# Layer 0 of a two-layer image kernel: the skip term and two products move to GpSimd

## The chip, the cores and the metric

The kernel runs on one core of one Trainium2 chip, in float32 throughout. The metric is the device time of one execution in microseconds (us). A core has TensorE (PE; its weight loads are listed apart as PEld), VectorE (DVE), ScalarE (ACT), GpSimd (POOL) and SyncE (SP), whose queue issues the DMAs. Each engine runs its own instructions in order; between engines, semaphores hold an instruction back until its data or its buffer is there.

## The reference, cut to what matters

The input is x, 8 images of 64 x 64 positions and 192 channels. Layer 0 normalizes it, applies a depthwise 3x3 convolution with a residual, a LayerNorm, a Mamba-2 style mixer (below), a second depthwise convolution, a LayerNorm and an MLP of width 768 with GELU; the result is added to x. Layer 1 is a selective scan in four directions over 384 channels and 16 states. Only layer 0's mixer is touched:

```python
xBC = silu(causal_conv1d(xBC, conv1d_w, conv1d_b))
xm = xBC[..., :DIN].reshape(B, L, NH, HD)      # 6 heads of 64
Bm, Cm = ...                                   # 64 states each
# inside a chunk, per head:
scores = (Cm_i . Bm_j) * exp(cs_i - cs_j) * dt_j   (j <= i)
y      = scores @ xm
states = sum_j Bm_j * (dt_j * decay_last_j) * xm_j
y      = y + (Cm @ carried state) * exp(cs)
y = y + xm * D_skip[None, None, :, None]
y = y.reshape(B, L, DIN) * silu(z)
```

## The kernel before

Layer 0 cuts each image's 4,096 positions into 8 tiles of 512 tokens, 64 tiles in all, and each tile into 4 chunks of 128 tokens. In most of layer 0 channels lie on partitions and tokens run along the free dimension; in the mixer tokens lie on partitions.

The order of the instructions is not written out by hand. Each stage is a Python generator (`mlp`, `norm2`, `conv2`, `output`, `mixer`, `states`, `turn`, `scores`, `powers` and so on) that yields steps with an engine and a cost (`step("DVE", 0.55, ...)`), takes and gives back buffers by name (`yield "take", "sm"`), and waits for events (`yield "wait", ("e", T, c)`). The planner `Flow` picks at every turn the step that could start soonest by those costs, plus a small rank per stage, and records it. The order that results is fixed on every engine. When a cost, a buffer or a step changes, the planner lays the whole of layer 0 in a new order; it knows nothing of engines that slow each other.

What stands around the change:

- `convolve` leaves `cv`, the 384 channels of xm for a tile, channels on partitions.
- `turn` (p_t, L698) transposes a chunk of `cv` by three PE transposes into a PSUM tile of the `sm` pool (3 buffers). DVE reads that tile twice: `xdt` = x*dt (L704) and `xw` = x*w (L709), with dt and w broadcast over the 64 columns of a head. Each has one buffer. Then the PSUM tile is given back.
- `states` multiplies the carried state with C (p_i, L739), scales it on DVE into `t1` (the trace calls it `t`, L741, one buffer), and makes the chunk's new state from `xw` (p_n, L750), with a decay and an add on DVE (L760, L763).
- `mixer` sums y in PSUM (p_y): three matmuls of `cv` with `dsk`, diagonal matrices of D (L786), then for each head a matmul of the scores `e` with `xdt` (L789). An fp32 matmul is two instructions in the trace. DVE adds `t1` (L802) and multiplies by silu(z) (`zs`, L805). The first chunk of an image has no carried state and no add.
- GpSimd holds the sums over two channel groups in the LayerNorms (`s`, L365), the residual sum `xr<-xr,x` (L923, one a tile) and small edge copies. DVE holds the two 3x3 convolutions (L343), 16 `scalar_tensor_tensor` instructions each per tile, and the causal convolution (L497), 12 per tile.

Layer 1 runs after layer 0 and shares nothing with it but the images in DRAM.

Of the kernel before, what the change touches and what calls it, by code (L numbers as in the profile page):

```python
# [8 lines left out]
F32 = mybir.dt.float32  # L9
# [13 lines left out]
NH, HD, NS = 6, 64, 64  # L23
DIN = 384
# [29 lines left out]
def bc(ap, axis, shape):  # L54

    return ap.unsqueeze(axis).to_broadcast(shape)
# [128 lines left out]
def step(engine, weight, do, after=None, table=None):  # L185
    return engine, weight, do, after, table


def layer0(tc, consts, x, x1s, mv1, w_in, w_out, w_fc1, w_fc2, rows):
    nc = tc.nc  # L190
    ident, low, up, grp, eps, ones96, ones1, p96, p128 = consts
    v96 = {k: p96[:, s] for k, s in C96.items()}
    v128 = {k: p128[:, s] for k, s in C128.items()}
# [8 lines left out]
    with ExitStack() as ctx:  # L202
# [32 lines left out]
        nc.vector.tensor_add(fb1, ps[:, 0:6], v128["fb1"])  # L235
        for ct in range(CT):
            nc.vector.tensor_scalar_mul(wf1[:, ct], wf1[:, ct], v96["l2w"][:, ct : ct + 1])
        rv = wp.tile([128, 12], F32, name="rv")
        nc.sync.dma_start(out=rv, in_=rows.partition_broadcast(128))
        dtb, an = rv[:, 0:6], rv[:, 6:12]  # L240
        nc.scalar.activation(an, an, AF.Exp)
        nc.vector.tensor_scalar_mul(an, an, -1.0)

        for i in range(3):
            nc.vector.tensor_scalar_mul(wo[:, i], wo[:, i], v128["rms"][:, i : i + 1])
        dsk = wp.tile([128, 3, 128], F32, name="dsk")
        for i in range(3):
            nc.vector.tensor_scalar_mul(dsk[:, i], ident, v128["dsk"][:, i : i + 1])

        xins = [wp.tile([CP, CT, RT + 2, WI + 2], F32, name=f"xin{i}") for i in range(2)]  # L250
        xxs = [xxp.tile([CP, CT, RT + 2, WI + 2], F32, name=f"xx{i}", bufs=1) for i in range(3)]
# [3 lines left out]
        f = Flow(tc)  # L255
        f.LAG, f.STAY, f.RANK = 0.684, -0.464, -0.01
        for tag, n in (("mm", 5), ("sm", 3), ("xin", 2), ("xs", 3), ("h", 3), ("cin", 2), ("cv", 2), ("zs", 2),
                       ("dt", 2), ("e", 5), ("yt", 4), ("yc", 1), ("xx", 3), ("x2", 1), ("m", 1), ("sq", 1), ("s2", 1), ("ld", 3), ("csr", 1), ("xdt", 1), ("xw", 1), ("t1", 1)):
            f.pool(tag, n)
        got = {}  # L260

# [422 lines left out]
        def turn():  # L684

            for T in range(len(tiles)):
                yield "wait", ("w2", T)
                yield "wait", ("cv", T)
                dt, w2, cv, bm = got["dt", T], got["w2", T], got["cv", T], got["bm", T]
                for c in range(NQ):  # L690
                    tk = slice(c * Q, c * Q + Q)
                    yield "take", "sm"
                    px = qp.tile([128, DIN], F32, name="p_t", tag="sm")
                    r = yield step(
                        "PE",
                        0.4,
                        lambda: [
                            nc.tensor.transpose(px[:, i * 128 : i * 128 + 128], cv[:, i, tk], ident) for i in range(3)  # L698
                        ],
                    )  # L700
                    yield "take", "xdt"
                    xdt = got["xdt", T, c] = ch.tile([128, DIN], F32, name="xdt", bufs=1)
                    f.at["xdt", T, c] = yield step(
                        "DVE", 0.55, lambda: [nc.vector.tensor_mul(hv(xdt), hv(px), bc(dt[:, c], 2, heads))], r  # L704
                    )
                    yield "take", "xw"
                    xw = got["xw", T, c] = ch.tile([128, DIN], F32, name="xw", bufs=1)
                    r = yield step(
                        "DVE", 0.55, lambda: [nc.vector.tensor_mul(hv(xw), hv(px), bc(w2[:, c], 2, heads))], r  # L709
                    )  # L710
                    f.give("sm", r)
                    yield "take", "sm"
                    pb = qp.tile([128, DIN], F32, name="p_b", tag="sm")
                    q = yield step("PE", 0.2, lambda: [nc.tensor.transpose(pb[:, :NS], bm[:, tk], ident[:NS, :NS])], 0.0)
                    f.fork(keep_b(T, c, pb, q, r))
# [52 lines left out]
        def mixer():  # L768

            for T, (b, t) in enumerate(tiles):  # L770
                yield "wait", ("cv", T)
                cv = got["cv", T]
                ssq = got["ssq", T] = sp.tile([128, NQ], F32, name="ssq")
                for c in range(NQ):
                    tk = slice(c * Q, c * Q + Q)
                    yield "wait", ("xdt", T, c)
                    yield "wait", ("e", T, c)
                    e, xdt = got.pop(("e", T, c)), got.pop(("xdt", T, c))
                    yield "take", "sm"
                    py = qp.tile([128, DIN], F32, name="p_y", tag="sm")  # L780

                    def out():

                        for i in range(3):
                            cs = slice(i * 128, i * 128 + 128)
                            f.keep(nc.tensor.matmul(py[:, cs], cv[:, i, tk], dsk[:, i], start=i == 0, stop=False))  # L786
                        for hd in range(NH):
                            cs = slice(hd * HD, hd * HD + HD)
                            f.keep(nc.tensor.matmul(py[:, cs], e[:, hd], xdt[:, cs], start=False, stop=hd == NH - 1))  # L789

                    q = yield step("PE", 2.2, out)
                    f.give("e", q)
                    f.give("xdt", q)
                    if c == 0:
                        yield "wait", ("zs", T)
                    zs = got["zs", T]
                    yield "take", "yt"
                    yt = got["yt", T, c] = tp.tile([128, DIN], F32, name="yt", bufs=4)
                    if t or c:
                        yield "wait", ("t1", T, c)  # L800
                        t1 = got.pop(("t1", T, c))
                        q = yield step("DVE", 0.55, lambda: [nc.vector.tensor_add(yt, t1, py)])  # L802
                        f.give("sm", q)
                        f.give("t1", q)
                        q = yield step("DVE", 0.66, lambda: [nc.vector.tensor_mul(yt, yt, zs[:, c])])  # L805
                    else:
                        q = yield step("DVE", 0.55, lambda: [nc.vector.tensor_mul(yt, py, zs[:, c])])
                        f.give("sm", q)
                    sqj = ch.tile([128, DIN], F32, name="sqj", bufs=1)
                    r = yield step(  # L810
                        "ACT",
                        0.75,
                        lambda: [nc.scalar.activation(sqj, yt, AF.Square, accum_out=ssq[:, c : c + 1])],
                        q,
                    )
                f.give("zs", q)
                yield "wait", ("states", T)
                f.give("cv", q)
                f.give("dt", q)
                f.at["yt", T] = r  # L820
# [1016 lines left out]
def _layout(i):  # L1837
    import numpy as np

    g = {k: np.asarray(a) for k, a in i.items()}  # L1840
    l0 = lambda k: g["L0_conv_" + k]
    l1 = lambda k: g["L1_conv_" + k]

    def part(a, p):

        a = a.reshape(-1, p, int(np.prod(a.shape[1:])))
        return a.transpose(1, 0, 2).reshape(p, -1)

    p96 = [l0(k) for k in ("cpe1_w", "cpe1_b", "ln1_w", "ln1_b", "cpe2_w", "cpe2_b", "ln2_w", "ln2_b", "fc2_b")]
    p128 = [l0("conv1d_w"), l0("conv1d_b"), l0("rms_w"), np.repeat(l0("D_skip"), HD), l0("fc1_b")]  # L1850
    p128 += [l1(k) for k in ("conv_w", "conv_b")]

    al = l1("A_logs").reshape(K, 2 * DT, 64, NP1, 2).transpose(4, 2, 0, 3, 1)
    p128 = [part(a, 128) for a in p128]
    p128 += [part(l1("Ds"), 128), al.reshape(128, -1), part(l1("ln_gamma"), 128), part(l1("ln_beta"), 128)]
    win = l0("in_proj_w")
    wx = l1("x_proj_weight")
    out = {
        "x": g["x"].transpose(0, 3, 1, 2).reshape(g["x"].shape[0], C, L),
        "p96": np.concatenate([part(a, CP) for a in p96], 1),  # L1860
        "p128": np.concatenate(p128, 1),
        "rows": np.concatenate([l0("dt_bias"), l0("A_log")]),

        "w_in0": np.concatenate([win[:384], win[896:], win[384:896]]).T,
        "w_out0": l0("out_proj_w").T,
        "w_fc1": l0("fc1_w").T,
        "w_fc2": l0("fc2_w").T,
        "w_in1": l1("in_proj_w").T,

        "w_x": np.concatenate([wx[:, R:], wx[:, :R]], 1).transpose(2, 0, 1),  # L1870
        "w_dt": np.concatenate([l1("dt_projs_weight").transpose(0, 2, 1), l1("dt_projs_bias")[:, None]], 1),
        "w_out1": l1("out_proj_w").T,
    }
    return {k: np.ascontiguousarray(a) for k, a in out.items()}
# [18 lines left out]
```

## Time and profile before

| What | Value |
| --- | --- |
| Median of 3 runs | 23,702.0 us (23,690.56 to 23,706.31) |
| Profiled execution | 23,706.3 us; its span is the same 23,706.3 us |
| PE busy over the span | 21,012.6 us (89%) |
| DVE busy over the span | 21,257.2 us (90%) |
| ACT busy over the span | 20,961.7 us (88%) |
| POOL busy over the span | 16,001.1 us (67%) |
| First and last transposes p_t of layer 0 | 94.6 us and 4,648.5 us |

A view by windows gives each engine's busy time in a stretch of the span, with the TensorE clock granted in it. A row of a group names the source line, the engine, the operation, what it writes and reads with its shapes, how often it occurred, its busy time in us and its mean in ns, and after the second bar the idle time of the engine just before it with what ended that idle time. Busy time counts overlapping instructions of one engine once, so the mean times the count can be larger. A row of the timeline begins with the start and the length in us.

### The profile page before, as it was taken

The page shows a single profiled execution, that of the slowest core. Times are in us where ns is not written, and L with a number is a line of the kernel's source. Part 1 is how long each engine was busy: PE and PEld are TensorE (multiplying, and loading weights), DVE is VectorE, ACT ScalarE, POOL GpSimd, SP SyncE. Part 2 cuts the span into 40 slices and gives each one's busy share as a digit, 9 for nine tenths or more (in the row PEclk, how much of TensorE's full clock was granted, in tenths as well). Part 3 has the DMA queues.
Part 4 walks back from the last instruction along what each step waited for, and adds up shares of the span by engine and source line. Part 5 has one row for each costly group of instructions (what it writes and reads, how often), then busy time and mean ns, then how long its engine had stood idle before and what let it go on. Part 6 is the DMA issues. An engine that isn't in the chain of part 4 may idle for free.

```text
span 23706.3 us, 312102 instructions
## 1 busy us (share of the span) xinstructions
PE 21012.6 (89%) x100356; PEld 10233.4 (43%) x100356; DVE 21257.2 (90%) x22093; ACT 20961.7 (88%) x37466; POOL 16001.1 (67%) x12871
## 2 busy tenths in 40 slices
PE   8999999978888888888888888888888888888888
PEld 4444444434444444444444444444444444444444
DVE  7888888779998999899989998999899989998998
ACT  5666666679998999899989998999899989998998
POOL 1111111159995998599859986997699769976997
PEclk8999999989999999999999999999999999999999
DMA  1111111133233322332233233322333333333332
GB/s 51 44 44 44 45 45 46 36 101 81 82 78 112 81 81 77 110 82 81 77 108 81 81 80 111 81 81 78 108 81 82 84 102 81 82 86 100 82 82 67
DMA packets 1205983, 1859.70 MB, mean 78 GB/s; under 512 B 268960, under 2 KB 502336, under 8 KB 1195136
## 3 DMA queue, kind: packets, MB, share of 16 engines
q1 hardware_dynamic: 1204352, 1839.73, 28.5%
q8 instruction: 807, 13.22, 0.2%
q14 instruction: 824, 6.75, 0.1%
HBM read 1225.98 MB, written 210.50 MB: 61 GB/s over the span
## 4 chain that ended last, share of the span: by engine, by line
POOL 46%; PE 22%; ACT 13%; DVE 8%; issue 6%; DMA 3%; SPq 1%; POOLq 0%; ACTq 0%; DVEq 0%
POOL hc L1647 43%; ACT pw L1591 5%; ACT ea L1606 5%; POOL cy L1645 3%; PE p_f L955 3%; DVE xs L1201 2%; DMA xc<-xo 2%; PE p_x L448 2%; PE p_f L975 2%; PE y L1662 2%; PE p_o L872 1%; PE g L1617 1%; PE p_y L789 1%; PE p_d L1480 1%; PE p_z L531 1%
## 5 line engine op out<-in xcount | busy, mean ns | idle before, releaser
L1647 POOL TENSOR_TENSOR hc<-hs,cb 128x1024 f32<-128x1024 f32 x6144 | 14577.6, 2373 | 12.3 <-POOL cy L1645 10.5
L1633 DVE TENSOR_TENSOR_SCAN hs<-ea,cy,g 128x512 f32<-128x512 f32 x10752 | 13027.1, 1262 | 602.4 <-PE g L1617 408.7
L1591 ACT ACTIVATE pw<-duT,bt 128x384 f32<-128x384 f32 x16384 | 8875.4, 601 | 23.5 <-DVE duT L1538 23.5
L1606 ACT ACTIVATE ea<-dr,an 128x512 f32<-128x512 f32 x12288 | 8121.7, 709 | 186.9 <-DVE hs L1633 169.5
L1662 PE MATMUL y<-hc,sel 128*64 128x512 f32 x24576 | 6628.6, 618 | 1836.3 <-POOL hc L1647 1816.1
L1617 PEld LDWEIGHTS g<-ident,pw 128*128 128x128 f32 x49152 | 5288.2, 141 | 4335.1 <-issue 2666.3
L1617 PE MATMUL g<-ident,pw 128*128 128x128 f32 x49152 | 6788.1, 279 | 60.8 <-ACT pw L1591 29.3
L1645 POOL COPY cy<-hs 128x2 f32<-128x2 f32 x6144 | 1150.7, 187 | 3394.4 <-DMA out_x<-xl 1744.8
L1662 PEld LDWEIGHTS y<-hc,sel 128*64 128x64 f32 x24576 | 1226.6, 135 | 3250.6 <-POOL hc L1647 3025.0
L1633 DVE TENSOR_TENSOR_SCAN hs<-ea,g 128x512 f32<-128x512 f32 x1536 | 1764.2, 1203 | 160.9 <-PE g L1617 119.6
L365 POOL TENSOR_TENSOR s<-xs 96x512 f32<-96x512 f32 x64 | 121.7, 1902 | 2136.0 <-DVE xs L343 1846.6
L1201 DVE SCALAR_TENSOR_TENSOR xs<-pad,p,xs 128x4096 f32<-128x4096 f32 x192 | 860.9, 4484 | 48.0 <-ACT xs L1191 40.8
L1509 PE MATMUL p_dt<-xdbl,wd 13*128 13x512 f32 x1536 | 857.5, 639 | 41.8 <-DVE de L1522 39.9
L365 POOL TENSOR_TENSOR s<-sq 96x512 f32<-96x512 f32 x128 | 180.4, 1409 | 937.9 <-ACT sq L378 842.3
L1480 PE MATMUL p_d<-xc,wx 128*44 128x512 f32 x1536 | 788.7, 596 | 23.4 <-DMA xc<-xo 23.4
L343 DVE SCALAR_TENSOR_TENSOR x<-xx,p,x 96x512 f32<-96x512 f32 x1024 | 784.4, 815 | 15.2 <-ACT x L332 15.0
L955 PE MATMUL p_f<-h,wf 96*128 96x512 f32 x1536 | 757.2, 631 | 43.8 <-ACT zs L550 27.4
L343 DVE SCALAR_TENSOR_TENSOR xs<-xin,p,xs 96x512 f32<-96x512 f32 x1024 | 746.9, 768 | 3.6 <-ACT xs L332 3.6
L975 PE MATMUL p_f<-m,wf 128*96 128x512 f32 x1536 | 695.0, 603 | 0.0
L1531 PEld LDWEIGHTS p_du<-ident,de 128*128 128x128 f32 x3072 | 323.4, 141 | 610.1 <-DVE de L1522 406.3
L365 POOL TENSOR_TENSOR s<-x 96x512 f32<-96x512 f32 x64 | 109.1, 1704 | 690.3 <-DVE x L343 606.7
L448 PE MATMUL p_x<-h,wi 96*128 96x512 f32 x1024 | 559.4, 679 | 12.0 <-ACT h L405 12.0
(202 smaller groups left out, 19293.3 us busy)
## 6 DMA issues: line engine op xcount, KB each, us to landing
cb<-cd SPq DMA_DIRECT2D x4096, 128.0 KB
dr<-de SPq DMA_DIRECT2D x3072, 128.0 KB
xc<-xo SPq DMA_DIRECT2D x256, 768.0 KB
e<-csd SPq DMA_DIRECT2D x256, 384.0 KB
xl<-x SPq DMA_DIRECT2D x256, 384.0 KB
ut<-xo SPq DMA_DIRECT2D x128, 768.0 KB
ut<-xo SPq DMA_DIRECT2D x256, 384.0 KB
xo<-xs SPq DMA_DIRECT2D x48, 1024.0 KB
```

The source lines that it names most:

```text
L343: nc.vector.scalar_tensor_tensor(im(out[:, ct]), tap(ct, j), w[:, ct, j : j + 1], im(out[:, ct]), ALU.mult, ALU.add)
L448: nc.tensor.matmul(ps, wi[:, ct, 390 + mt * 128 : 518 + mt * 128], h[:, ct], start=ct == 0, stop=ct == 1)
L955: nc.tensor.matmul(ps, wf1[:, ct, mt * 128 : mt * 128 + 128], h[:, ct], start=ct == 0, stop=ct == 1)
L975: nc.tensor.matmul(ps[:CP], wf2[:, kt, ct * CP : ct * CP + CP], m[:, kt], start=kt == 0, stop=kt == 5)
L1201: nc.vector.scalar_tensor_tensor(xs, tap(j), kw[:, d, j : j + 1], xs, ALU.mult, ALU.add)
L1591: nc.scalar.activation(st["pw", p, j][:, :, i], st["duT"][:, j].rearrange("p (g c) -> p g c", c=64), AF.Copy, scale=st["bt"][:, j, n : n + 1],
L1606: nc.scalar.activation(ea[:, f], state[s]["dr", d][:, f], AF.Exp, scale=an[:, k, p, at : at + 1])
L1617: nc.tensor.transpose(g[:, f, j * 128 : j * 128 + 128], state[s]["pw", p, j][:, 2 * d + f].rearrange("p a b -> p (a b)"), ident,)
L1633: nc.vector.tensor_tensor_scan(rev(h[:, f]), rev(ea[:, f]), rev(g[:, f]), 0.0 if first(s) else state[s - 1]["cy"][:, p, d, f : f + 1], ALU ...
L1645: o(nc.gpsimd.tensor_copy(st["cy"][:, p, d], h[:, :, last]))
L1647: o(nc.gpsimd.tensor_mul(hc, h, bc(st["cb", p], 1, [128, 2, TT])))
L1662: o(nc.tensor.matmul(y[half[f]], sel, hc[:, f], start=p == 0 and k > 0, stop=p == NP1 - 1))
```

## The change

The transposed chunk is copied once from PSUM by ScalarE into a new SBUF tile `xr` (two buffers; the name also belongs to an unrelated tile of the second LayerNorm stage). The PSUM tile is given back after that copy. GpSimd forms `xw` and then `xdt` from `xr`, then multiplies `xr` by D in place. In `mixer` the three diagonal matmuls are gone and each head's matmul starts its own sum; GpSimd adds `t1` to `xr`, and DVE adds `xr` to the PSUM tile. The first chunk of an image now has that add as well. D is loaded as 6 further values of the broadcast row vector, and the diagonal matrices `dsk` are not built.

```diff
@@ -235,17 +235,14 @@
         nc.vector.tensor_add(fb1, ps[:, 0:6], v128["fb1"])
-        rv = wp.tile([128, 12], F32, name="rv")
+        rv = wp.tile([128, 18], F32, name="rv")
         nc.sync.dma_start(out=rv, in_=rows.partition_broadcast(128))
-        dtb, an = rv[:, 0:6], rv[:, 6:12]
+        dtb, an, skip = rv[:, 0:6], rv[:, 6:12], rv[:, 12:18]
         nc.scalar.activation(an, an, AF.Exp)
         nc.vector.tensor_scalar_mul(an, an, -1.0)
 
         for i in range(3):
             nc.vector.tensor_scalar_mul(wo[:, i], wo[:, i], v128["rms"][:, i : i + 1])
-        dsk = wp.tile([128, 3, 128], F32, name="dsk")
-        for i in range(3):
-            nc.vector.tensor_scalar_mul(dsk[:, i], ident, v128["dsk"][:, i : i + 1])
 
         xins = [wp.tile([CP, CT, RT + 2, WI + 2], F32, name=f"xin{i}") for i in range(2)]
         xxs = [xxp.tile([CP, CT, RT + 2, WI + 2], F32, name=f"xx{i}", bufs=1) for i in range(3)]
@@ -255,7 +252,7 @@
         f = Flow(tc)
         f.LAG, f.STAY, f.RANK = 0.684, -0.464, -0.01
         for tag, n in (("mm", 5), ("sm", 3), ("xin", 2), ("xs", 3), ("h", 3), ("cin", 2), ("cv", 2), ("zs", 2),
-                       ("dt", 2), ("e", 5), ("yt", 4), ("yc", 1), ("xx", 3), ("x2", 1), ("m", 1), ("sq", 1), ("s2", 1), ("ld", 3), ("csr", 1), ("xdt", 1), ("xw", 1), ("t1", 1)):
+                       ("dt", 2), ("e", 5), ("yt", 4), ("yc", 1), ("xx", 3), ("x2", 1), ("m", 1), ("sq", 1), ("s2", 1), ("ld", 3), ("csr", 1), ("xdt", 1), ("xw", 1), ("t1", 1), ("xr", 2)):
             f.pool(tag, n)
         got = {}
 
@@ -698,17 +695,23 @@
                             nc.tensor.transpose(px[:, i * 128 : i * 128 + 128], cv[:, i, tk], ident) for i in range(3)
                         ],
                     )
+                    yield "take", "xr"
+                    xr = got["xr", T, c] = ch.tile([128, DIN], F32, name="xr", bufs=2)
+                    r = yield step("ACT", 0.5, lambda: [nc.scalar.copy(xr, px)], r)
+                    f.give("sm", r)
+                    yield "take", "xw"
+                    xw = got["xw", T, c] = ch.tile([128, DIN], F32, name="xw", bufs=1)
+                    r = yield step(
+                        "POOL", 1.0, lambda: [nc.gpsimd.tensor_mul(hv(xw), hv(xr), bc(w2[:, c], 2, heads))]
+                    )
                     yield "take", "xdt"
                     xdt = got["xdt", T, c] = ch.tile([128, DIN], F32, name="xdt", bufs=1)
                     f.at["xdt", T, c] = yield step(
-                        "DVE", 0.55, lambda: [nc.vector.tensor_mul(hv(xdt), hv(px), bc(dt[:, c], 2, heads))], r
-                    )
-                    yield "take", "xw"
-                    xw = got["xw", T, c] = ch.tile([128, DIN], F32, name="xw", bufs=1)
-                    r = yield step(
-                        "DVE", 0.55, lambda: [nc.vector.tensor_mul(hv(xw), hv(px), bc(w2[:, c], 2, heads))], r
-                    )
-                    f.give("sm", r)
+                        "POOL", 1.0, lambda: [nc.gpsimd.tensor_mul(hv(xdt), hv(xr), bc(dt[:, c], 2, heads))], 0.0
+                    )
+                    f.at["xr", T, c] = yield step(
+                        "POOL", 1.0, lambda: [nc.gpsimd.tensor_mul(hv(xr), hv(xr), bc(skip, 2, heads))], 0.0
+                    )
                     yield "take", "sm"
                     pb = qp.tile([128, DIN], F32, name="p_b", tag="sm")
                     q = yield step("PE", 0.2, lambda: [nc.tensor.transpose(pb[:, :NS], bm[:, tk], ident[:NS, :NS])], 0.0)
@@ -781,14 +784,11 @@
 
                     def out():
 
-                        for i in range(3):
-                            cs = slice(i * 128, i * 128 + 128)
-                            f.keep(nc.tensor.matmul(py[:, cs], cv[:, i, tk], dsk[:, i], start=i == 0, stop=False))
                         for hd in range(NH):
                             cs = slice(hd * HD, hd * HD + HD)
-                            f.keep(nc.tensor.matmul(py[:, cs], e[:, hd], xdt[:, cs], start=False, stop=hd == NH - 1))
-
-                    q = yield step("PE", 2.2, out)
+                            f.keep(nc.tensor.matmul(py[:, cs], e[:, hd], xdt[:, cs], start=True, stop=True))
+
+                    q = yield step("PE", 1.3, out)
                     f.give("e", q)
                     f.give("xdt", q)
                     if c == 0:
@@ -796,16 +796,17 @@
                     zs = got["zs", T]
                     yield "take", "yt"
                     yt = got["yt", T, c] = tp.tile([128, DIN], F32, name="yt", bufs=4)
+                    yield "wait", ("xr", T, c)
+                    xr = got.pop(("xr", T, c))
                     if t or c:
                         yield "wait", ("t1", T, c)
                         t1 = got.pop(("t1", T, c))
-                        q = yield step("DVE", 0.55, lambda: [nc.vector.tensor_add(yt, t1, py)])
-                        f.give("sm", q)
+                        q = yield step("POOL", 1.0, lambda: [nc.gpsimd.tensor_add(xr, xr, t1)])
                         f.give("t1", q)
-                        q = yield step("DVE", 0.66, lambda: [nc.vector.tensor_mul(yt, yt, zs[:, c])])
-                    else:
-                        q = yield step("DVE", 0.55, lambda: [nc.vector.tensor_mul(yt, py, zs[:, c])])
-                        f.give("sm", q)
+                    q = yield step("DVE", 0.55, lambda: [nc.vector.tensor_add(yt, xr, py)])
+                    f.give("sm", q)
+                    f.give("xr", q)
+                    q = yield step("DVE", 0.66, lambda: [nc.vector.tensor_mul(yt, yt, zs[:, c])])
                     sqj = ch.tile([128, DIN], F32, name="sqj", bufs=1)
                     r = yield step(
                         "ACT",
@@ -1859,7 +1860,7 @@
         "p96": np.concatenate([part(a, CP) for a in p96], 1),
         "p128": np.concatenate(p128, 1),
-        "rows": np.concatenate([l0("dt_bias"), l0("A_log")]),
+        "rows": np.concatenate([l0("dt_bias"), l0("A_log"), l0("D_skip")]),
 
         "w_in0": np.concatenate([win[:384], win[896:], win[384:896]]).T,
         "w_out0": l0("out_proj_w").T,
```

## The prediction

> **What bounds the kernel now.** The change touches layer 0 only, so I first cut layer 0 out of the span. In the page's forty slices GpSimd jumps from 1 tenth to 5 and then 9 at the ninth and tenth: layer 0 fills the first eight slices, about 4,700 us of 23,706, and the rest is layer 1, where GpSimd's `hc` products carry the chain of waits (43%). Nothing of layer 1 is edited, so the stake is what a layer-0 tile takes, 64 times over.
>
> ```profile
> POOL 1111111159995998599859986997699769976997
> ```
>
> Second, the busy time by windows, over 3,600 us of even running inside layer 0. The columns are length, then busy us (and instructions) of PE, PEld, DVE, ACT, POOL, then the granted clock.
>
> ```profile
> 900.00:4500.00 3600.00, 3368.48 (x11474) 1659.46 (x11472) 2994.53 (x4989) 2411.98 (x4737) 498.93 (x413) 0.94 0.17 45
> ```
>
> Third, the groups of the same window with shapes kept apart.
>
> ```profile
> L343 DVE SCALAR_TENSOR_TENSOR x<-xx,p,x 96x512 f32<-96x512 f32 x800 | 615.6, 819 | 0.0
> L786 PE MATMUL p_y<-dsk,cv 128*128 128x128 f32 x1188 | 181.4, 291 | 7.1 <-DVE gm L676 6.5 <-ACT yc L858 0.6
> L365 POOL TENSOR_TENSOR s<-sq 96x512 f32<-96x512 f32 x100 | 142.3, 1423 | 715.4 <-ACT sq L378 652.1 <-PE p_u L849 25.9 <-PE p_g L672 21.1
> L923 POOL TENSOR_TENSOR xr<-xr,x 96x1024 f32<-96x1024 f32 x50 | 127.6, 2552 | 0.0
> L704 DVE TENSOR_TENSOR xdt<-p_t,dt 128x384 f32<-128x384 f32 x198 | 109.2, 551 | 260.1 <-PE p_y L789 260.1
> L709 DVE TENSOR_TENSOR xw<-p_t,w 128x384 f32<-128x384 f32 x197 | 107.5, 546 | 9.8 <-PE p_n L750 9.8
> L858 ACT COPY yc<-p_u 128x384 f32<-128x384 f32 x200 | 94.0, 470 | 112.7 <-PE p_u L849 112.1
> ```
>
> The tile sum `xr<-xr,x` occurs 50 times, once a tile, so a tile (4 chunks of 128 tokens) takes 3600/50 = **72.0 us**. Per tile PE is busy 67.4 us, DVE 59.9, ACT 48.2, POOL 10.0. PE idles 4.6 us a tile: it is the bound, at 0.936 of the time. DVE has 12.1 us to spare, of which 260.1/50 = 5.2 is the wait of `xdt` for the p_y matmul that still reads its only buffer.
>
> Fourth, the timeline of one stretch, for what DVE and POOL do to each other.
>
> ```profile
> 2529.89 2.81 POOL L365 TENSOR_TENSOR s<-x 96x512 f32<-96x512 f32 x1 [6.04 <-DVE x L343]
> 2531.50 2.02 DVE L681 TENSOR_TENSOR e<-e,gm 128x768 f32<-128x768 f32 x1
> 2536.21 0.94 DVE L681 TENSOR_TENSOR e<-e,gm 128x768 f32<-128x768 f32 x1
> ```
>
> The same `e*gm` takes 2.02 us while the GpSimd sum runs and 0.94 us with GpSimd idle; the sum itself takes 2.81 us where the fastest in the window takes 1.26. They exclude each other.
>
> **What the Trainium skill says.** "SBUF — State Buffer", section Who interferes with whom: a DVE instruction with two SBUF inputs contends with a GpSimd instruction that reads SBUF, and the later one blocks fully; a DVE instruction with at most one SBUF input is free of it. The trace agrees. Of the 800 `x` steps of the convolution (two SBUF inputs), 616 meet no GpSimd instruction and average 737 ns; the 102 that start while one runs average 1,368. The `xdt` product (one input in PSUM) takes 551 ns alone and 552 during GpSimd work. "GPSIMD Engine Reference", section 3.1, prices a two-input elementwise product at about 2.6 cycles an element at 1.2 GHz: an estimate of 384 x 2.6 / 1.2 = 0.83 us before overhead. Its section 1 gives GpSimd no PSUM access, which is why the copy by ScalarE has to exist; no run here shows that.
>
> **The change, part by part.** The profiled execution took 23,706.3 us, which is also its span (nothing lies around it), 4.3 above the median of 23,702.0. Sums are per tile, then times 64.
>
> PE loses 6 instructions a chunk (three 128-column matmuls, two passes each). The group's 181.4 us over 198 chunks is 0.92 us a chunk, but it overlaps its neighbours: from the first of the six to the first `e` matmul is 0.67 us in the median and 0.75 on average. I take 0.75: 3.0 us a tile, 192 us in all. Ends: 0.67 (172) and 0.92 (235). PE becomes 64.4 us.
>
> DVE loses `xdt` and `xw`. From the start of one to the start of what follows back to back is 0.467 us: 8 x 0.467 = 3.7 us a tile. The eight image-first chunks gain one add (4 us in all), and three setup instructions of 0.27 us go; both count as nothing, and no cover is needed. The 5.2 us wait for the `xdt` buffer moves to POOL's queue. It was free time of an engine that was not the bound, so I credit nothing for it.
>
> ACT gains 4 copies out of PSUM; `yc` has the same shape at 470 ns: 1.9 us. The planner's new order also holds 363 table loads instead of 319; 44 x 1.283 us / 64 = 0.9 us. ACT becomes 51.0 of 72 us; idle time covers it. Without that cover it would cost 2.8 x 64 = 179 us. The queued work behind a copy that waits for the transpose is the next decays; 21 us a tile absorb that.
>
> POOL gains `xw`, `xdt`, the skip product and the add of `t1`: 256 x 3 + 248 = 1,016 instructions, 15.9 a tile. No 128x384 product exists on POOL before. The undisturbed minima, 1.258 us for 512 elements and 2.336 for 1,024, give a slope of 2.1 ns and a fixed 0.18: **0.99 us** at 384. The page's price with that overhead gives 1.01. The broadcast operand is new; I allow 0.9 to 1.3. So POOL gets 15.7 us more, 26 of 72 before its waits: far from full.
>
> What matters is what those 15.7 us do to DVE. DVE's two-SBUF-input work is 2,142/50 = 42.8 us a tile undisturbed, POOL's existing work 8.2: together 51 of 72 us on the shared reads, after the change 67. Existing POOL work lengthens DVE instructions by 140 us over the 50 tiles, 0.34 of its own 8.2 us. By kind the share is 0.46 (`s<-sq`, released by ACT, like the new products), 0.54 (`s<-xs`), 0.33 (`xr`), 0.14 (`s<-x`). I take 0.5: 7.9 us a tile. Ends: 0.14 (2.2 us) and all (15.7). **DVE becomes 59.9 - 3.7 + 7.9 = 64.1 us** (58.4 to 71.9), as full as PE. So the change does not move work to an idle engine: 3.7 us leave DVE and about 8 come back as blocking.
>
> The new waits. `p_n` and `p_y` now wait for POOL, behind which the whole PE queue stands. By row durations the new PE order has a median of 14.5 us of PE work between a chunk's transposes and its `p_n` (lowest tenth 7.8), 16 us to `p_y`. The chain copy, `xw`, `xdt` needs 0.47 + 2 x 0.99 us and up to one 0.94 us block each, some 4 to 5 us. It is covered unless POOL's queue is stuck: the products stand in order behind `s<-xs`, which already waits 1,394.7 us in 42 waits for DVE's convolution, some 33 us each. DVE's `yt` add now waits for POOL's add of `t1`; median DVE work between them is 7.0 us, lowest tenth 3.0, against about 2 us needed, so only a few stall. The PSUM slot of the transposes is freed after one copy instead of two products, slightly earlier. The reload of the `rows` vector by 6 values, the only altered DMA, is nothing; SP's queue has no new transfer. All other instructions move, since the planner lays the whole order again from the new costs.
>
> **Putting it together.** The old 0.936 of PE held while DVE had 12 us of slack. With two engines at 64 us that block each other I take PE's busy share at 0.88, its idle share nearly doubled. That is a choice, not a measurement: 64.4/0.88 = 73.2 us a tile, 1.2 more, 77 us in all: 23,783. At 0.895 the change would be neutral.
>
> **The rivals.**
> *A, the saving lands:* DVE is blocked little because products fall on its one-input work or idle time, PE keeps 0.936, so 64.4/0.936 = 68.8 us, 3.2 less, 205 us in all: 23,501. For it: the 3,368 busy us of PE, DVE's 5.2 us of buffer wait, the 10 us of PE work that hides the POOL chain. Against it: 42.8 us a tile of exclusive DVE work.
> *B, balance:* the forecast, 23,783; its own range 23,620 to 23,930.
> *C, the shared read interface is the bound:* nearly every POOL product holds up DVE, DVE needs 71.9 us, and at the 0.936 that a bounding engine reaches here a tile takes 76.8 us, 4.8 more: +307 us, 24,013. It decides from a blocked share of about 0.75, where DVE reaches 68 us; queued products behind a blocked `s<-xs` push the same way. For it: 0.54 on `s<-xs`, 67 of 72 us on the interface. Against it: the average of 0.34.
> That the change does not take effect is excluded: the new order has 1,536 instead of 3,072 p_y matmuls and the 1,016 GpSimd ones.
>
> **The numbers.** What a measurement of this kernel can tell from no change is about 0.2%, 47 us. A has 0.27 (0.26 faster, 0.01 same), B 0.46 (0.04 faster, 0.13 same, 0.29 slower), C 0.27, all slower. Faster 0.30, same 0.14, slower 0.56. Cases of both signs hold the chance, so B's own range stands above; the range over all, 23,510 to 24,090, leaves a tenth at each end: a full A with 0.92 us a chunk, and a C with POOL products of 1.3 us.
>
> **What would show each step.** Right: over the same window of layer 0, tiles of about 73 us, PE's busy share down to 0.88, POOL's 128x384 products near 1.0 to 1.3 us, the `x` steps of the convolution above their 819 ns mean at 900 or more, DVE's busy time up although two products left it, layer 1 unchanged. Wrong: DVE busy under 59 us a tile (A), or over 68 (C); PE waiting long on `xw` or `xdt` would put the loss in POOL's queue and not in the reads.

## The result and the profile after

The changed kernel takes 23,833.36 us in the median of 4 runs (23,820.16 to 23,848.16) against 23,704.15 for the kernel before beside it: a ratio of 1.0055, 95% interval 1.0042 to 1.0069, or **129 us slower**. The forecast was 23,783, 77 us slower.

The time is lost in layer 0. From the first transposes to the last a tile takes (4,648.5 - 94.6)/63 = 72.3 us before and (4,814.4 - 95.1)/63 = 74.9 us after; the last transposes come 166 us later, the first `hc` product of layer 1 137 us later, the end 128 us later. The end of layer 0 and layer 1 give some of it back, and the rows of layer 1 are the same within a few us.

The window of 900 to 4,500 us after, with the columns as before (length, busy us and count of PE, PEld, DVE, ACT, POOL, then the granted clock):

```profile
900.00:4500.00 3600.00, 3290.65 (x9961) 1556.93 (x9959) 2961.64 (x4447) 2447.74 (x4802) 1564.45 (x1155) 0.89 0.16 43
```

The slices of GpSimd over the span, in tenths:

```profile
POOL 3444444439995999599959995998599869976997
```

GpSimd's share of layer 0 went from 0.14 to 0.43. At 74.9 us a tile the window holds 48.1 tiles: PE is busy 68.5 us of each, DVE 61.6, ACT 50.9, POOL 32.6. PE lost six instructions a chunk and is *busier* than before; the granted clock in the same row, 0.94 before and 0.89 here, says why.

The groups of that window, shapes kept apart, that answer to those shown of before:

```profile
L340 DVE SCALAR_TENSOR_TENSOR x<-xx,p,x 96x512 f32<-96x512 f32 x766 | 631.5, 876 | 0.0
L362 POOL TENSOR_TENSOR s<-sq 96x512 f32<-96x512 f32 x96 | 154.2, 1606 | 199.7 <-ACT sq L375 180.3 <-DVE x L340 9.3 <-PE p_u L850 6.5
L705 POOL TENSOR_TENSOR xw<-xr,w 128x384 f32<-128x384 f32 x191 | 366.4, 1918 | 684.0 <-PE p_n L753 428.7 <-ACT xr L700 207.0 <-DVE t L744 27.0
L710 POOL TENSOR_TENSOR xdt<-xr,dt 128x384 f32<-128x384 f32 x191 | 249.0, 1304 | 358.5 <-PE p_y L789 358.4
L804 POOL TENSOR_TENSOR xr<-xr,t 128x384 f32<-128x384 f32 x186 | 237.8, 1278 | 161.7 <-DVE t L744 156.3 <-DVE dr L544 4.3
L700 ACT COPY xr<-p_t 128x384 f32<-128x384 f32 x190 | 90.6, 477 | 188.9 <-DVE yt L806 88.1 <-PE p_t L695 86.7 <-DVE dr L544 7.9
L713 POOL TENSOR_TENSOR xr<-xr,rv 128x384 f32<-128x384 f32 x191 | 212.3, 1111 | 13.6
L806 DVE TENSOR_TENSOR yt<-xr,p_y 128x384 f32<-128x384 f32 x192 | 104.7, 546 | 209.4 <-POOL xr L804 193.3 <-PE p_u L850 8.5 <-PE p_f L956 6.1
L789 PE MATMUL p_y<-xdt,e 128*128 128x64 f32 x2304 | 323.3, 296 | 21.4 <-DVE e L678 10.7 <-POOL xdt L710 7.1 <-DVE st L766 1.3
```

The convolution's steps went from a mean of 819 to 876 ns. The new products and the add take 1.1 to 1.9 us on average, where the shortest product takes 0.82 and the shortest add 0.98. GpSimd now waits for PE, 428.7 us for `p_n` to free `xw` and 358.4 us for `p_y` to free `xdt`, and DVE waits 193.3 us for GpSimd's add. PE itself hardly waits for the products (7.1 us for `xdt`). The timeline of one stretch shows how those last two link (start and length in us, the wait in brackets):

```profile
2501.96 0.83 POOL L710 TENSOR_TENSOR xdt<-xr,dt 128x384 f32<-128x384 f32 x1 [7.73 <-PE p_y L789]
2502.87 0.83 POOL L713 TENSOR_TENSOR xr<-xr,rv 128x384 f32<-128x384 f32 x1
2503.66 1.26 POOL L362 TENSOR_TENSOR s<-x 96x512 f32<-96x512 f32 x1
2504.88 0.99 POOL L804 TENSOR_TENSOR xr<-xr,t 128x384 f32<-128x384 f32 x1
2505.90 0.56 DVE L806 TENSOR_TENSOR yt<-xr,p_y 128x384 f32<-128x384 f32 x1 [3.58 <-POOL xr L804]
...
2522.03 2.80 POOL L924 TENSOR_TENSOR xr<-xr,x 96x1024 f32<-96x1024 f32 x1
...
2522.54 5.48 DVE L494 SCALAR_TENSOR_TENSOR cv<-cin,p,cv 128x512 f32<-128x512 f32 x5
```

GpSimd stands 7.73 us for the `xdt` buffer, then works through its queue, and DVE stands 3.58 us for the add at the end of it. Below, five convolution steps, the first of them held up by the GpSimd sum above it, take 5.48 us; at the 0.66 us from start to start that they show undisturbed they take some 3.4.

The blocking falls on GpSimd too, and harder. In another stretch one product meets a row of DVE's two-input instructions:

```profile
2651.11 10.10 POOL L705 TENSOR_TENSOR xw<-xr,w 128x384 f32<-128x384 f32 x1 [0.84 <-ACT xr L700]
...
2651.62 0.94 DVE L678 TENSOR_TENSOR e<-e,gm 128x768 f32<-128x768 f32 x1
2652.49 3.39 DVE L340 SCALAR_TENSOR_TENSOR xs<-xin,p,xs 96x512 f32<-96x512 f32 x5
2655.80 0.74 DVE L494 SCALAR_TENSOR_TENSOR cv<-cin,p,cv 128x512 f32<-128x512 f32 x1
2656.47 0.74 DVE L340 SCALAR_TENSOR_TENSOR xs<-xin,p,xs 96x512 f32<-96x512 f32 x1
2657.13 3.39 DVE L494 SCALAR_TENSOR_TENSOR cv<-cin,p,cv 128x512 f32<-128x512 f32 x5
```

A two-input instruction of DVE (`h*rs`) was running when the product began. The thirteen shown start after it, none of them is lengthened, and the product ends 0.7 us after the last of them: 10.10 us instead of 0.82. Over the window, products and adds take 413 us more than their shortest times, 8.6 us a tile.

### The profile page after: what moved, and what is told of

The parts are those of the page before. It is cut to its first block, busy times and chain, and to the rows that moved or that the text cites. A ratio compares the mean times of both kernels' runs of the same rounds, so it can differ in the third digit from the quotient of the medians.

```text
span 23834.7 us, 310291 instructions
## 1 busy us (share of the span) xinstructions
PE 21029.7 (88%) x98820; PEld 10147.4 (43%) x98820; DVE 21334.5 (90%) x21586; ACT 21123.1 (89%) x37766; POOL 17450.2 (73%) x13887
## 4 chain that ended last, share of the span: by engine, by line
POOL 46%; PE 20%; ACT 14%; DVE 9%; issue 7%; DMA 3%; SPq 1%; POOLq 0%; ACTq 0%; DVEq 0%
POOL hc L1648 41%; ACT pw L1592 6%; ACT ea L1607 5%; POOL cy L1646 3%; DVE xs L1202 2%; PE p_f L956 2%; DMA xc<-xo 2%; PE y L1663 2%; PE p_f L976 2%; PE p_o L873 1%; PE g L1618 1%; PE p_d L1481 1%; PE p_x L445 1%; DVE xs L340 1%; PE p_o L1408 1%
## 5 line engine op out<-in xcount | busy, mean ns | idle before, releaser
L705 POOL TENSOR_TENSOR xw<-xr,w 128x384 f32<-128x384 f32 x256 | 464.3, 1814 | 912.5 <-PE p_n L753 589.4
L340 DVE SCALAR_TENSOR_TENSOR x<-xx,p,x 96x512 f32<-96x512 f32 x1024 | 840.8, 871 | 11.5 <-ACT x L329 11.5
L340 DVE SCALAR_TENSOR_TENSOR xs<-xin,p,xs 96x512 f32<-96x512 f32 x1024 | 837.2, 854 | 12.9 <-ACT xs L329 12.9
L710 POOL TENSOR_TENSOR xdt<-xr,dt 128x384 f32<-128x384 f32 x256 | 338.3, 1322 | 443.0 <-PE p_y L789 437.7
```

The lines of the kernel that those rows point to most:

```text
L340: nc.vector.scalar_tensor_tensor(im(out[:, ct]), tap(ct, j), w[:, ct, j : j + 1], im(out[:, ct]), ALU.mult, ALU.add)
```

## The experiments

All differences are against the kernel before, timed beside them (23,703 to 23,704 us). "Lengthening" is what DVE's instructions take above the undisturbed time of their own kind while a GpSimd instruction runs, summed over the window and given per tile: 2.8 us before, 7.8 after. Where it is divided among GpSimd's instructions, it is put to the one already running when DVE's began. A tile is the distance from the first transposes to the last, over 63.

**PE's part alone.** `D*x` is left out of the result. In `mixer` (each head's matmul then starts its own sum, as in the change):

```diff
-                        for i in range(3):
-                            cs = slice(i * 128, i * 128 + 128)
-                            f.keep(nc.tensor.matmul(py[:, cs], cv[:, i, tk], dsk[:, i], start=i == 0, stop=False))
```

> The kernel before without the three diagonal matmuls (D*x is left out of the result), with the planner's costs kept, so that every engine's order is the old one otherwise. If PE's busy time bounds layer 0 at an unchanged clock, the 0.75 us a chunk come back whole: 256 x 0.75 = 192 us, about 23,510 us. If something else sets the pace as soon as PE is relieved, or PE's granted clock falls when it has more gaps, less than a third comes back: above 23,640 us, and the mean granted clock in 900 to 4,500 us lies below 0.94.

Measured 23,638.98: -64 us (0.9971, 0.9959 to 0.9983), a third of the 192. Its window:

```profile
900.00:4500.00 3600.00, 3362.77 (x10435) 1574.27 (x10435) 3024.89 (x5062) 2443.45 (x4811) 522.52 (x417) 0.92 0.17 45
```

PE is as busy as before (3,363 us against 3,368) at a lower clock. The clock records know two values here, full and half. PE's busy time at half clock rose from 7.4 to 10.5 us a tile, and its work in full-clock time (its busy time less half of that at half clock) fell from 63.9 to 61.3. So about 2.6 us of work went and half of the 3.1 us more at half clock, 1.5, came back as longer matmuls: the tile is 1.0 us shorter, 71.3 us.

**GpSimd products alone, and GpSimd writes alone**, both in the old order. Two at each of two places a chunk:

```diff
+        idle_pool = lambda: [nc.gpsimd.tensor_mul(hv(cd), hv(ca), bc(dtb, 2, heads)) for _ in range(2)]
...
-                        "DVE", 0.55, lambda: [nc.vector.tensor_mul(hv(xdt), hv(px), bc(dt[:, c], 2, heads))], r
+                        "DVE", 0.55, lambda: [nc.vector.tensor_mul(hv(xdt), hv(px), bc(dt[:, c], 2, heads))] + idle_pool(), r
...
-                        q = yield step("DVE", 0.55, lambda: [nc.vector.tensor_add(yt, t1, py)])
+                        q = yield step("DVE", 0.55, lambda: [nc.vector.tensor_add(yt, t1, py)] + idle_pool())
```

> The kernel before, complete, with four more GpSimd products of 128x384 a chunk (two SBUF inputs, constants, a tile that nothing reads) in the old order; nothing waits for them. Theory of the shared reads: they hold up DVE's two-input instructions by about half of their 0.99 us, 7.9 us a tile; DVE has 12 us of slack, so between +100 and +400 us (23,800 to 24,100). Theory of the waits (what costs time is that PE and DVE wait for GpSimd's results in a new order): within 60 us of before, DVE lengthened by no more than 3 us a tile.

```diff
+        idle_pool = lambda: [nc.gpsimd.memset(cd, 0.0) for _ in range(3)]
```

> The same places as in the run with added products, but six GpSimd memsets of 128x704 a chunk, which take GpSimd about as long (estimated from the 204 ns for 132 elements and 108 ns for 12: some 0.65 us each, 3.9 us a chunk) and read nothing. Theory of the shared reads: no DVE instruction is lengthened more than before, the time is within 60 us of before. If it is only GpSimd's queue, late with its LayerNorm sums, that costs time: as slow as the run with the products.

The products cost **+261 us** (1.0109, 1.0095 to 1.0122), the memsets **+43** (1.0019, 1.0012 to 1.0025), at nearly the same GpSimd time. The GpSimd group and the convolution's group, first with products, then with memsets:

```profile
L632 POOL TENSOR_TENSOR cdum<-wo,rv 128x384 f32<-128x384 f32 x737 | 836.2, 1135 | 41.8
L345 DVE SCALAR_TENSOR_TENSOR x<-xx,p,x 96x512 f32<-96x512 f32 x752 | 618.4, 872 | 0.0
```

```profile
L631 POOL MEMSET cdum<- 128x704 f32 x1158 | 791.5, 683 | 54.4
L344 DVE SCALAR_TENSOR_TENSOR x<-xx,p,x 96x512 f32<-96x512 f32 x784 | 601.9, 818 | 0.0
```

With products the convolution step averages 872 ns, with memsets 818, where it was 819. The memsets hold up DVE by about 2 us in the whole window, the products by about 170. Lengthening rises to 7.0 us a tile with products, 3.4 with memsets. So 218 us is the price of GpSimd's *reads* in the old order, where nothing waits for the results. With products a tile grows by 3.9 us for 4.2 us of lengthening: nearly one for one, although DVE had 12 us of idle time a tile.

**Two buffers.** In the changed kernel (to make room, the `rs` tile of the LayerNorms has one buffer instead of two):

```diff
-                    xw = got["xw", T, c] = ch.tile([128, DIN], F32, name="xw", bufs=1)
+                    xw = got["xw", T, c] = ch.tile([128, DIN], F32, name="xw", bufs=2)
...
-                    xdt = got["xdt", T, c] = ch.tile([128, DIN], F32, name="xdt", bufs=1)
+                    xdt = got["xdt", T, c] = ch.tile([128, DIN], F32, name="xdt", bufs=2)
```

> The changed kernel with two buffers each for xw and xdt (and one instead of two for the rs tile of the LayerNorms, to make room). Theory of the waits: GpSimd no longer stands 429 and 358 us in the window waiting for p_n and p_y, the adds of t1 behind come earlier, DVE's 193 us of waiting for them shrinks under 80; 60 to 130 us come back: 23,700 to 23,775 us. Theory of the shared reads: as many products collide as before, 23,800 to 23,870 us.

Measured 23,846.70: +144 us (1.0060, 1.0047 to 1.0072), no better than the change. DVE's waits in its window (waits, times, longest):

```profile
DVE gm L673 <- PE p_g L669: 112.5, 65, 5.9
DVE t L744 <- PE p_i L742: 109.6, 64, 8.5
...
DVE yt L806 <- POOL xr L804: 25.6, 13, 4.9
```

The wait for the add falls from 193.3 to 25.6 us, as the theory of the waits wants, and the time does not follow: waits for PE grow (`gm` from 67 to 113, `t` from 49 to 110) and lengthening rises to 8.5 us. GpSimd's waits for `p_n` and `p_y` are gone, but it now waits 640.6 us for ScalarE's copy, 207.0 in the change. Ending the wait for these buffers did not help by itself. The order was laid anew here too and `rs` lost a buffer, so this says nothing finer.

**The order alone.** In the kernel before, `step("PE", 2.2, out)` becomes `step("PE", 1.3, out)`.

> The kernel before with one number altered: the planner's cost of the p_y step is 1.3 instead of 2.2, while its matmuls, the diagonal ones among them, stay. Only the order is laid anew. If the re-laid order by itself is what costs the changed kernel its time, this run loses 60 us or more (23,760 us and above). If the reads cost it, the time is within 60 us of before, 23,640 to 23,760.

Measured 23,954.32: **+250 us** (1.0103, 1.0087 to 1.0118), with not one instruction of work changed. A single planning number can cost twice what the whole change cost.

**Half of the change.** `xdt` and, in the same way, `xw` stay on DVE:

```diff
-                        "POOL", 1.0, lambda: [nc.gpsimd.tensor_mul(hv(xdt), hv(xr), bc(dt[:, c], 2, heads))], 0.0
+                        "DVE", 0.55, lambda: [nc.vector.tensor_mul(hv(xdt), hv(px), bc(dt[:, c], 2, heads))], r
```

> Half of the change: ScalarE copies, GpSimd forms the skip product and adds t1, the diagonal matmuls are gone, but DVE keeps xdt and xw out of PSUM, which don't touch the shared reads. GpSimd gets 8 instructions a tile instead of 16, DVE gets its 3.7 us back. Theory of the shared reads (218 us for 16 products in the old order, 1.0 us less a tile of PE worth 64): half the collisions, about +110 - 64 = +45, 23,700 to 23,800 us. Theory that relief of DVE is what the change has going for it: 3.7 us more on DVE at full price, 23,850 us and above.

Measured 23,907.18: +203 us (1.0084, 1.0070 to 1.0098). With half of GpSimd's work, lengthening 5.8 instead of 7.8 us, it is slower than the whole change. DVE's 3.7 us are back, but a new order is in this number too.

**PE's work put back into the change,** as idle matmuls that the sum of `p_y` overwrites; the order is the changed kernel's own.

```diff
+                        for i in range(3):
+                            cs = slice(i * 128, i * 128 + 128)
+                            f.keep(nc.tensor.matmul(py[:, cs], cv[:, i, tk], ident, start=True, stop=True))
                         for hd in range(NH):
```

> The changed kernel in its own order with three idle 128x128 matmuls a chunk put back in front of the p_y sum, which overwrites them: PE's work of before is there again, everything else is the change. If PE's time counts fully: +192 us, about 24,025 us. If PE's clock gives back two thirds of what it is spared, as the run without the diagonal suggests (its time at half clock rose from 7.4 to 10.6 us a tile): +30 to +100 us, 23,865 to 23,935, with the granted clock higher than the changed kernel's 0.89.

Measured 23,827.17: 6 us *below* the change, within the spread of its runs (+123 over before; 1.0051, 1.0038 to 1.0063). Both theories expected a loss; there is none. Its window:

```profile
900.00:4500.00 3600.00, 3336.48 (x11144) 1661.23 (x11144) 2946.39 (x4461) 2457.41 (x4823) 1542.17 (x1160) 0.92 0.16 43
```

PE did 64.0 us of full-clock work a tile instead of 61.2, but spent 10.4 instead of 14.5 us at half clock. So in the changed kernel's order the work of the diagonal matmuls costs nothing.

**DVE's products twice.** In the kernel before, both products `for _ in range(2)`.

> The kernel before with xdt and xw each formed twice on DVE, the order kept: 8 x 0.467 = 3.7 us more a tile for DVE, with one operand in PSUM, so nothing touches the shared reads. This is what the change takes from DVE, doubled instead of removed. If DVE's 12 us of idle time a tile were slack: within 60 us of before. If DVE's time is on the path (the added products cost 3.9 us a tile for 4.2 us of lengthening): +150 to +260 us, 23,850 to 23,960.

Measured 23,962.29: **+258 us** (1.0108, 1.0094 to 1.0121). 3.7 us more of DVE make a tile 4.0 us longer:

```profile
900.00:4500.00 3600.00, 3298.68 (x10915) 1609.54 (x10914) 3063.61 (x5133) 2295.95 (x4502) 464.28 (x390) 0.92 0.16 43
```

At 76.2 us a tile DVE is idle for 11.4 us, hardly less than the 12.2 before, while PE's idle time grew from 4.7 to 6.4. DVE's idle time was no slack for this work. It does stand in the chain to `p_n` and `p_y`, so it delays results as well as filling DVE; the products on GpSimd, which lengthen DVE's instructions elsewhere, cost nearly one for one too.

**The change in the old order.** Its instructions issued from the steps of before:

```diff
-                        "DVE", 0.55, lambda: [nc.vector.tensor_mul(hv(xdt), hv(px), bc(dt[:, c], 2, heads))], r
+                        "DVE", 0.55, lambda: [
+                            nc.scalar.copy(xr, px),
+                            nc.gpsimd.tensor_mul(hv(xdt), hv(xr), bc(dt[:, c], 2, heads)),
+                        ], r
...
-                        q = yield step("DVE", 0.55, lambda: [nc.vector.tensor_add(yt, t1, py)])
+                        q = yield step("DVE", 0.55, lambda: [nc.gpsimd.tensor_add(xr, xr, t1), nc.vector.tensor_add(yt, xr, py)])
```

> All of the change's work (copy by ScalarE, xdt, xw, skip product and add on GpSimd, no diagonal matmuls), but issued from the kernel before's planned steps with their costs, so that each surviving instruction keeps its old place. Theory of the re-laid order: the mechanism by itself is about even, 1.3 us a tile more on DVE (+84 us) and PE's 64 us less, so 23,640 to 23,770 us, below the changed kernel's 23,833. Theory of the reads and of the waits for GpSimd: as slow as the changed kernel or slower, 23,800 us and above, with DVE's waits for the t1 add over 150 us in the window.

Measured 24,010.63: **+306 us** (1.0127, 1.0113 to 1.0141). The theory that the re-laid order made the loss finds no support: the same work costs more in the old order than in its own. The old order was not laid for it, though: the copy and the products stand where DVE's products stood, `xdt` ahead of `xw`, and no step counts their time on ScalarE or GpSimd. DVE's longest wait in the window, and the window itself:

```profile
DVE yt L804 <- POOL xr L804: 387.9, 127, 7.6
```

```profile
900.00:4500.00 3600.00, 3247.97 (x9669) 1518.24 (x9669) 2791.86 (x4318) 2322.44 (x4622) 1355.22 (x1129) 0.88 0.16 42
```

DVE is busy 59.7 us of a 77.0 us tile and waits 8.3 for GpSimd's add, which stands behind a queue that waits for `p_y` (499.2 us in the window) and for ScalarE's copy (400.8). Lengthening is 5.9 us.

**Another order for the change.** The same number set back from 1.3 to 2.2 in the changed kernel.

> The changed kernel with the planner's cost of the p_y step at 2.2 as before instead of 1.3; only its order is laid anew. If an order by itself is worth as much as the 250 us that this number moved in the kernel before, the time differs from the changed kernel's 23,833 us by more than 60 us, either way. If the changed kernel's time is set by its operations, 23,775 to 23,890 us.

Measured 23,829.82: +125 us (1.0051, 1.0039 to 1.0064), the change's time again.

**A way round GpSimd.** Still with the diagonal matmuls, in the old order: `xw`, then both products, on ScalarE, for each:

```diff
-                        "DVE", 0.55, lambda: [nc.vector.tensor_mul(hv(xw), hv(px), bc(w2[:, c], 2, heads))], r
+                        "DVE", 0.55, lambda: [
+                            nc.scalar.activation(
+                                xw[:, h * HD : h * HD + HD], px[:, h * HD : h * HD + HD], AF.Copy, scale=w2[:, c, h : h + 1]
+                            )
+                            for h in range(NH)
+                        ], r
```

> The kernel before, diagonal matmuls and all, in its own order, with xw formed by ScalarE from PSUM (six activations of 64 columns with the head's w as the scale, about 0.2 us each) instead of by DVE. DVE loses 1.9 us a tile and nothing collides with GpSimd. DVE's time counts about one for one (theory of DVE on the path): -120 us, 23,540 to 23,620. If PE is the bound after all: within 60 us of before. ScalarE gains 4.9 us a tile of its 24 idle ones; if its order can't take that, slower than before.

> As the run with xw on ScalarE, with xdt there too: DVE loses 3.7 us a tile, as in the change, without any collision with GpSimd; ScalarE gains 9.8 us a tile. DVE on the path: -200 to -260 us, 23,440 to 23,510. If ScalarE, now at 58 of 72 us, takes over as the late one: between 23,600 and 23,800.

Measured 23,827.87: +123 us (1.0051, 1.0037 to 1.0064), and 23,926.70: +222 us (1.0093, 1.0079 to 1.0106). Both missed: relief of DVE did not pay in this order. ScalarE's group in the first:

```profile
L710 ACT ACTIVATE xw<-p_t,w 128x64 f32<-128x64 f32 x1170 | 260.8, 323 | 315.6 <-DVE xdt L704 272.9 <-PE p_n L755 35.6 <-DVE gn_v L80 6.8
```

ScalarE now stands 272.9 us behind DVE's `xdt`, which itself waits for `p_y`; in the second it stands 340.8 us for `p_y` directly. A wait that DVE bore went to ScalarE's queue; that this costs the time is likely, not shown. In all 256 chunks `xw` starts only after DVE's `xdt` has ended, by 0.03 us or more, although both only read the PSUM tile; what imposes that order is not known. The planner still counted these steps as DVE's, so an order laid for ScalarE was not tried.

No version beats the kernel before, except the one that leaves D*x out.

## Why the prediction was right, and where not

**The direction held, and its cause as far as the runs reach.** The forecast said that GpSimd's products would block DVE's two-input instructions and turn a saving into a loss. The runs with products and memsets show that the reads alone can do it, at 218 us in the old order; in the changed kernel's own order their share stays open. This is what "SBUF — State Buffer" in the Trainium skill says in Who interferes with whom, and here it has a price: GpSimd instructions that only write held up DVE by about 2 us in 3,600. The trace after shows the exclusion: of the 270 `x` steps that start while a two-input GpSimd instruction runs, 166 end in the median 0.55 us after it. The other 104 take their undisturbed 0.74 us while GpSimd's instruction lasts on.

**The blocked share was too large.** I took 0.5 for the products. Measured over undisturbed product time, it is 0.26 to 0.30 in the changed kernel, and 0.28 for the added products. Lengthening grew by 5.0 us a tile instead of 7.9: 3.8 from the new products and add, the rest from GpSimd's older sums, which now hold DVE up more than before. DVE is busy 61.6 us instead of 64.1, and the convolution's steps take 876 ns, not the 900 or more that the forecast named as a sign. The products were also shorter undisturbed, 0.82 us where one operand is broadcast, 0.98 for the add, against the 0.99 taken for all.

**What DVE's blocking costs was too small,** and this is the step that failed: of PE, "it is the bound", with 12.1 us of DVE "to spare". Adding 3.7 us to DVE costs 4.0 us a tile; taking 2.6 us of work from PE gains 1.0, and in the changed kernel giving it back costs nothing. So PE's 94% did not make it the bound by itself; work was added to PE only in the changed kernel, not in the kernel before. Nor is DVE a plain bound, for moving its products to ScalarE cost time. The engines wait for each other in fixed orders: work added to DVE shows nearly in full, work taken from PE in part, work moved from DVE to ScalarE as a loss.

**PE's saving of 192 us did not arrive.** The work went (2.7 us a tile at full clock); the forecast had it fall through to time, at an unchanged clock. From before to after PE's time at half clock doubled, 7.4 to 14.5 us a tile, which makes its matmuls 3.5 us longer. "TensorE: Matmul & The Clock Gate" in the Trainium skill, Part 1, says that the array's clock halves when PE has been idle and returns after a busy stretch. The records agree, at 0.5 or 1.0 only, with one difference: PE need not be idle. Their 54 half-clock stretches before and 71 after last multiples of 3.4 us. In the 3.4 us ahead of each PE was busy 45% of the time before and 47% after, in the median; in the 3.4 us ahead of the return, 100%. So waits that leave PE half empty for that long are followed by a lower clock. Whether the clock cost time of its own or only filled gaps that other waits had opened is not shown.

**The waits were underrated.** The forecast gave GpSimd's `xw` and `xdt` "up to one 0.94 us block each", as if the later instruction had to wait for one DVE instruction. The 10.10 us above show that DVE's instructions which came later went ahead, one after another. A tenth of the `xw` products take over 4.4 us, and GpSimd is busy 22.6 us a tile more, not 15.7. Of the waits for the add the forecast said that "only a few stall": DVE waits 193 us in the window for the add, 4.0 us a tile, and 8.3 in the old order. The 5.2 us wait for the `xdt` buffer, which I let go with its move to GpSimd, came back as 358 us there. Yet two buffers removed it and most of the 193 us without gain.

**So the 0.88** that I chose for PE's share stands at 68.5/74.9 = 0.91, and the sum came near (77 against 129 us) partly by luck, with errors of both signs: too much blocking, too much saving, too little price. Rival A fell with its bound on PE. Rival C, DVE at over 68 us, did not happen. The re-laid order, which I counted at nothing, fits the change better than the old one: 306 us there, 129 in its own. One count in the forecast is wrong, without effect on it: the matmuls of `p_y` go from 2,304 to 1,536 (4,608 instructions to 3,072), not from 3,072.

**Open:** how the 129 us divide between reads, waits and clock in the changed kernel's own order. Each run that removes one of them there also lays the order anew, except the one with PE's work put back.

## What to carry to other kernels

An engine that is busy 94% of a stretch is not thereby its bound: add a known amount of idle work to each engine in turn, off the chain of results where possible, keep the order, and see which one moves the time. Before work goes to GpSimd, count the neighbour's instructions with two SBUF inputs, and test with products and memsets of equal length whether its reads or its queue cost. Where a planner lays the order, an experiment needs the old order as its control, for here one cost number was worth 250 us.

## What was not expected of the hardware

A float32 product of 128x384 with one operand broadcast over 64 columns takes 0.82 us on GpSimd, an add of two full tiles 0.98. A memset of 128x704 takes 0.68 us and leaves DVE undisturbed. A GpSimd product can wait through thirteen later DVE instructions with two SBUF inputs, 10.10 us in all. On PE, removing 2.6 us of work a tile raised the time at half clock by 3.1 us; putting 2.8 us back into the changed kernel lowered it by 4.1.
